# Four-layer residual sequence kernel: the output of the state-space layer and the LSTM's first input group of the next chunk stand one step later in each pass

## The chip, the cores and the metric

The kernel runs on one core of a Trainium2 chip. The metric is device time in microseconds (us). The engines are TensorE (PE; its weight loads are listed on their own as PEld), VectorE (DVE), ScalarE (ACT), GpSimd (POOL) and SyncE (SP), which issues transfers. Each engine takes its own instructions in their written order and waits at semaphores for the others.

## The reference

Four residual layers follow each other on `x` of 4 sequences, 1024 positions, width 512. A conditioning vector per sequence, `cond`, enters layers 0, 1 and 3 and is the start state of layers 0 and 2:

```
x = x + RNN(x, h0=cond)              # h = tanh(x Wx0 + h Wh0), 1024 steps
x = x + SSM(x, cond)                 # short convolution over 4 positions, then
                                     # state = decay*state + dt*B_t*u_t ; y = C_t*state ; y @ Wo + bo
x = x + LSTM(x, h0=cond, c0=0)       # A = x Wx2 + h Wh2 ; i,f,o = sigmoid, g = tanh
                                     # c = f*c + i*g ; h = o*tanh(c), 1024 steps
x = x + x @ (base + lowrank(cond))   # one matrix per sequence
```

The two recurrences make the time serial: the LSTM has 1024 steps, and each needs the state of the one before.

## The kernel before, in words

**Passes and steps.** Positions are cut into 32 chunks of 32. One pass of `do_pass` (line 815) carries the LSTM through the 32 steps of chunk c, while the RNN runs 56 steps ahead of it (`LEAD`). Into the same steps are spread the state-space layer of chunk c+1 (`ssm_jobs`), the RNN's input projection of chunk c+3 (`project0`), the last layer of chunk c-1 (`adapt_jobs`), and the LSTM's input projection (`input_jobs`). The order is written by hand: nothing reorders it.

**The LSTM step.** The hidden width is cut into half A (m = 0) and half B (m = 1). The 96 weight loads and matmuls of `lstm_mm` (line 383; the state is what is loaded, the bfloat16 parts of the weights stream) come in this order: contraction half 0 for A (24), a part for B (8), contraction half 1 for A (24), the rest for B (40). Contraction half 0 reads the state that half A made in the step before; contraction half 1, which begins with the 33rd load, reads the state that half B made. On DVE and ACT follow, per half: `transpose` and `transpose_o` (DVE, 402), `sum` and `sum_o` (DVE, 408), `gates` and `gate_o` (ACT, 415), `products` (DVE, 428), `cell` (DVE, 433), `tanh` (ACT, 438), `h` (DVE, 441) and two `split`s (DVE, 207) that make the lower parts of the state for the bfloat16 products. The `sum` takes in the input projection of the step, which `lstm_input` (ACT, line 390, one copy per half) brings from `xw2` into the tile `tt2` one step ahead.

**The slots.** Around this, each step has three places for other jobs. "pe" is on TensorE between `lstm_mm` and the RNN's matmuls `rnn_mm` (352). "gap" is after B's `cell`, ahead of the two copies of `lstm_input`, of B's `tanh`, `h` and `split`s. "end" is after these and after the RNN's `rnn_pre` (DVE, 367, 368) and `rnn_h` (ACT, 371). So the written order of a step ends like this:

```
Bh.cell()                      # DVE 433
do(t, "gap")
lstm_input(next step, m=0); lstm_input(next step, m=1)     # ACT 390
Bh.tanh()                      # ACT 438
Bh.h(); Bh.split(1); Bh.split(2)                           # DVE 441, 207
rnn_pre(); rnn_h()
do(t, "end")
```

A job is a tuple of step, slot and function. In step 31 the "next step" is step 0 of the next chunk.

**The jobs around the change.** The state-space layer's chain of DVE operations ends with `y` (line 521) in the "end" slot of step 23. `out_mm` (16 matmul calls at line 307 through `tiled`, with 64 contraction rows, out `ssm_out`, bank "po") multiplies it by `Wo`; `x2_end` (DVE, 533, four pieces) adds bias and residual into `x2`, the LSTM's input. `act.copy` (541) keeps the last three positions of `x1` for the next chunk. `input_jobs(c + 1, 0, ...)` then projects `x2` for steps 0 to 7 of the next chunk: four groups of matmuls (`input_mm`, 333, bank "ada"), two turns into `xw2` (`input_turn`, DVE, 337, one for gate groups 0 and 1, one for 2 and 3), and two additions of the bias in place (`input_bias`, DVE, 345, likewise). `lstm_input` reads `xw2` after that. The groups n = 1, 2, 3 for steps 8 to 31 are made inside the chunk's own pass.

Of the kernel before, what the change touches and what calls it, by code (L numbers as in the profile page):

```python
# [16 lines left out]
KC = D // P  # L17
TC = 32
# [21 lines left out]
def cond_resid_kernel(ctx: ExitStack, tc: tile.TileContext, a: dict, out: bass.AP):  # L40
# [410 lines left out]
    def ssm_jobs(c):  # L451
        x, h, po = xin[c % XBUFS], h0[c % 2], {}
        v, act = nc.vector, nc.scalar

        def sm(name):
            return small.tile([NS, TOK], F32, name=name, tag=name, bufs=1)

        def add(ms, t0, t1):
            t = lambda y: y[:, ms, t0:t1].rearrange("p c t b -> p c (t b)")
            v.tensor_add(t(x1[:, :, 3:, :]), t(x), t(h))  # L460


        jobs = [
            (5, "end", lambda: add(slice(0, 2), 0, TC - 4)),
            (6, "end", lambda: add(slice(2, 4), 0, TC - 4)),
            (7, "end", lambda: add(slice(0, 4), TC - 4, TC)),
        ]
        pb = bank("pb", [P, 2, TOK], tag="pb", bufs=1)


        def taps(k):
            for tap in range(TAPS):
                tiled(
                    pb[:, 0, :], lambda j: wp[:, tap, k, CT * j : CT * (j + 1)], x1[:, k, tap : tap + TC, :],
                    tap == 0 and k == 0, tap == TAPS - 1 and k == KC - 1,
                )

        def skip():
            for k in range(KC):
                tiled(  # L480
                    pb[:, 1, :], lambda j: ws[:, k, CT * j : CT * (j + 1)], x1[:, k, 3:, :],
                    k == 0, k == KC - 1, tiles=NS // CT,
                )

        cg, z, e, u, w, p = (sm(n) for n in ("cg", "z", "e", "u", "w", "p"))
        bt, vv, states, y = z, e, w, p
        v3, y3 = (t.rearrange("p (t b) -> p t b", b=B) for t in (vv, states))
        y_last = y3[:, TC - 1, :]
        jobs += [(8 + 2 * k, "pe", lambda k=k: taps(k)) for k in range(KC)]
        jobs.append((16, "pe", skip))  # L490

        def turn(n):
            cols = slice(n * TOK // 4, (n + 1) * TOK // 4)
            v.reciprocal(u[:, cols], u[:, cols])


        jobs += [
            (14, "end", lambda: act.activation(z, pb[:NS, 0, :], AF.Identity, bias=vec[:NS, 0:1])),
            (14, "end", lambda: act.activation(e, pb[:NS, 0, :], AF.Abs, bias=vec[:NS, 0:1])),
            (15, "end", lambda: act.activation(e, e, AF.Exp, scale=-1.0)),  # L500
            (15, "end", lambda: act.activation(u, e, AF.Copy, bias=2.0)),
            (18, "end", lambda: act.activation(cg, pb[NS:, 0, :], AF.Tanh, bias=vec[NS:, 0:1])),
            (18, "end", lambda: v.tensor_mul(u, u, e)),
            (18, "end", lambda: v.tensor_mul(w, u, u)),
            (18, "end", lambda: act.activation(p, w, AF.Copy, scale=2.0 * SERIES[-1])),
            (24, "end", lambda: act.copy(s1, y_last)),
        ]

        chain = [lambda q=q: v.scalar_tensor_tensor(p, p, 2.0 * q, w, ALU.add, ALU.mult) for q in SERIES[-2::-1]]
        chain += [  # L510
            lambda: v.scalar_tensor_tensor(p, p, 2.0, u, ALU.add, ALU.mult),
            lambda: v.scalar_tensor_tensor(bt, z, 0.0, p, ALU.max, ALU.add),
            lambda: v.scalar_tensor_tensor(vv, pb[:NS, 1, :], vec[:NS, 1:2], bt, ALU.add, ALU.mult),
        ]
        for b in range(B):
            chain.append(lambda b=b: v.tensor_tensor_scan(
                y3[:, :, b], decay, v3[:, :, b], s1[:, b : b + 1], ALU.mult, ALU.add
            ))

        chain += [  # L520
            lambda: v.scalar_tensor_tensor(y, states, dt, cg, ALU.mult, ALU.mult),
        ]
        place = lambda n: ("gap", "end", "end")[n % 3]
        jobs += [((16, "end"), (16, "end"), (17, "gap"), (17, "end"))[n] + (lambda n=n: turn(n),) for n in range(4)]
        jobs += [(19 + (n + 1) // 3, place(n + 1), f) for n, f in enumerate(chain)]

        def out_mm():
            po[0] = bank("ssm_out", [P, KC, TOK], tag="po", bufs=1)
            for m in range(KC):
                tiled(po[0][:, m, :], lambda j: wo[:, P * j + CT * m : P * j + CT * (m + 1)], y)  # L530

        def x2_end(m):
            v.scalar_tensor_tensor(
                x2[c % 2][:, m].rearrange("p t b -> p (t b)"), po[0][:, m, :], bo[:, 0, m : m + 1],
                x1[:, m, 3:, :].rearrange("p t b -> p (t b)"), ALU.add, ALU.add,
            )

        jobs += [
            (24, "pe", out_mm),
            *((24 + (m + 1) // 2, ("end", "gap")[m % 2], lambda m=m: x2_end(m)) for m in range(KC)),  # L540
            (26, "end", lambda: act.copy(x1[:, :, 0:3, :], x1[:, :, TC : TC + 3, :])),
        ]
        return jobs

# [270 lines left out]
    def do_pass(c, first=0, src=None, dst=None, last=None):  # L815

        lstm = c >= 0
        jobs = []
        if dst is not None:
            jobs += adapt_jobs(c - 1, dst)  # L820
        if c == NCHUNK - 1:
            more, rest = last_adapt(c, last)
            jobs += more
        if -1 <= c < NCHUNK - 1:
            jobs += ssm_jobs(c + 1)
            jobs += input_jobs(
                c + 1, 0, range(25, 29), ((28, "end"), (29, "gap"), (29, "end"), (30, "gap"))
            )
        if src is not None:
            jobs.append((9, "end", lambda: load_x(c + 4, src)))  # L830
        if c + 3 < NCHUNK:
            for m in range(KC):
                mm, end = project0(c + 3, m)
                t = (18, 20, 22, 30)[m]
                jobs += [(t, "pe", mm), (t, "end", end)]
        if lstm:
            jobs += input_jobs(c, 1, range(4), ((3, "end"), (4, "gap"), (4, "end"), (5, "gap")))
            jobs += input_jobs(c, 2, range(4, 8), ((8, "gap"), (8, "end"), (9, "gap"), (9, "end")))
            jobs += input_jobs(c, 3, range(9, 17, 2), ((15, "end"), (16, "gap"), (18, "gap"), (19, "gap")))

        def do(t, place):
            for slot, where, f in jobs:
                if (slot, where) == (t, place):
                    f()

        for t in range(first, TC):
            r = divmod(c * TC + t + LEAD, TC)
            rnn = r[0] < NCHUNK
            if lstm:
                A, Bh = Half(c, t, 0), Half(c, t, 1)  # L850
                lstm_mm(c, t, 0, 0)
                lstm_mm(c, t, 0, 1, (0, 1))
                lstm_mm(c, t, 1, 0)
                lstm_mm(c, t, 0, 1, (2, 3, 4, 5))
                lstm_mm(c, t, 1, 1)
            do(t, "pe")
            if rnn:
                rnn_mm(*r)
            if c * TC + t < 8 - TC:
                keep_busy()  # L860
            if lstm:
                A.transpose()
                A.sum()
                A.transpose_o()
                A.sum_o()
                A.gates()
                A.products()
                A.gate_o()
                Bh.transpose()
                A.cell()  # L870
                Bh.transpose_o()
                A.tanh()
                Bh.sum()
                Bh.gates()
                A.h()
                Bh.sum_o()
                A.split(1)
                Bh.gate_o()
                Bh.products()
                A.split(2)  # L880
                Bh.cell()
            do(t, "gap")
            if lstm:
                if (c, t) != (NCHUNK - 1, TC - 1):
                    for m in range(2):
                        lstm_input(c if t + 1 < TC else c + 1, (t + 1) % TC, m)
                Bh.tanh()
                Bh.h()
                Bh.split(1)
                Bh.split(2)  # L890
            if rnn:
                rnn_pre(*r)
                rnn_h(*r)
            do(t, "end")
            while later:
                later.pop()()
            for f in early.pop((c, t), ()):
                f()
        if last is not None:
            rest()  # L900
# [78 lines left out]
```

## Time and profile before

| | |
|---|---|
| time, median of 3 runs | 4686.77 us (4686.28 to 4688.5) |
| time of the profiled execution | 4682.72 us |
| span of the profiled execution, first to last instruction | 4680.9 us |
| busy PE / PEld / DVE / ACT / POOL | 4546.1 / 3574.0 / 3951.6 / 1876.8 / 47.9 us |
| granted TensorE clock, mean | 0.998 of full speed |
| DMA, mean over the span | 14 GB/s |

The profiled execution's time is its span and 1.82 us around it. It lies 4.05 us below the median of the runs. Busy time counts instructions that overlap in the pipelines, so a busy PE isn't PE at its peak. The start of half A's `transpose` (line 402, shape 128x192, the first of two such in a step) marks a step in the timeline: from one to the next is the length of the step.

### The profile page before, as it was taken

Reading aid. Unit: us, or ns where it says so; the run is one execution under the profiler, and the core shown is the slowest. Engines: PE = TensorE matmul, PEld = TensorE weight load, DVE = VectorE, ACT = ScalarE, POOL = GpSimd, SP = SyncE. Lnnn points to the kernel's source line nnn. Section 1 sums busy time; section 2 is a strip of 40 time slices with the busy share of each in tenths; the row PEclk is TensorE's granted clock in tenths of the full one; section 3 lists DMA queues with packets and bytes.
Section 4 is the critical chain, followed back from the end, with each engine's and each line's share of the span. In section 5 each row is a group of like instructions: output and inputs, shape, how many; then the busy total and the mean of one; then the engine's idle time right before and its main releaser. Section 6 shows DMA issues by size and latency. Waiting matters only on the chain.

```text
span 4680.9 us, 326427 instructions
## 1 busy us (share of the span) xinstructions
PE 4546.1 (97%) x146816; PEld 3574.0 (76%) x146816; DVE 3951.6 (84%) x22102; ACT 1876.8 (40%) x9693; POOL 47.9 (1%) x92
## 2 busy tenths in 40 slices
PE   7999999999999999999999999999999999999986
PEld 4777777777777777777777777778777777777754
DVE  4688888888888888888888888888888888888876
ACT  3334444444443444443444444444444444444333
POOL 3000000000000000000000000000000000000000
PEclk9999999999999999999999999999999999999999
DMA  6300000000000000000000000000000000000000
GB/s 151 123 6 8 9 7 9 9 7 9 9 7 9 9 7 9 9 7 9 9 7 9 9 7 9 9 7 9 9 7 9 9 7 9 9 5 7 6 6 8
DMA packets 40235, 67.77 MB, mean 14 GB/s; under 512 B 8864, under 2 KB 26016, under 8 KB 38320
## 3 DMA queue, kind: packets, MB, share of 16 engines
q1 hardware_dynamic: 35792, 46.55, 3.7%
q8 instruction: 1147, 18.79, 1.7%
q14 instruction: 256, 2.10, 0.2%
q0 software_dynamic: 1696, 0.19, 0.0%
q10 hardware_dynamic: 1344, 0.14, 0.0%
HBM read 38.34 MB, written 8.39 MB: 10 GB/s over the span
## 4 chain that ended last, share of the span: by engine, by line
PE 91%; DVE 7%; issue 1%; POOL 0%; DMA 0%; ACT 0%; SPq 0%; DVEq 0%; ACTq 0%; POOLq 0%
PE acc L383 55%; PE acc L352 18%; PE proj L333 9%; PE pb L307 3%; DVE tt L402 3%; DVE gc L408 2%; PE proj L307 2%; PE ada L754 2%; DVE prod L428 1%; PE ssm_out L307 1%; DVE h L207 1%; PE idle L307 0%; PE pp L615 0%; DVE h L441 0%; DVE tt L367 0%
## 5 line engine op out<-in xcount | busy, mean ns | idle before, releaser
L383 PE MATMUL acc<-wh,h 128*12 128x256 bf16 x98304 | 2900.4, 273 | 95.0 <-DVE h L207 92.0
L383 PEld LDWEIGHTS <-h 128*12 128x12 bf16 x98304 | 2312.5, 87 | 545.5 <-DVE h L207 181.9
L402 DVE STREAM_TRANSPOSE tt<-acc 128x192 f32<-128x192 f32 (+1 forms) x4096 | 1233.0, 309 | 285.9 <-PE acc L383 261.5
L415 ACT ACTIVATE gc<-gc 128x24 f32<-128x24 f32 (+1 forms) x4096 | 855.3, 216 | 1386.1 <-DVE gc L408 1379.4
L352 PEld LDWEIGHTS acc<-wh,h 128*4 128x4 f32 x32768 | 808.3, 87 | 507.3 <-issue 204.6
L352 PE MATMUL acc<-wh,h 128*4 128x128 f32 x32768 | 1088.6, 273 | 17.3 <-ACT h L371 12.8
L408 DVE TENSOR_REDUCE gc<-tt 128x24 f32<-128x96 f32 (+1 forms) x4096 | 1037.4, 255 | 70.5
L207 DVE TENSOR_TENSOR h<-h 128x8 f32<-128x8 f32 (+1 forms) x4098 | 671.6, 164 | 69.9
L371 ACT ACTIVATE h<-pre 128x16 f32<-128x16 f32 x1024 | 221.5, 216 | 1126.1 <-DVE pre L368 1126.1
L438 ACT ACTIVATE th<-gc 128x8 f32<-128x8 f32 x2048 | 427.7, 209 | 255.1 <-DVE gc L433 220.1
L333 PE MATMUL proj<-wx,x 128*32 128x512 f32 x4096 | 529.6, 592 | 0.0
L441 DVE SCALAR_TENSOR_TENSOR h<-gc,th 128x8 f32<-128x8 f32 x2048 | 328.5, 160 | 143.6 <-ACT th L438 134.0
L367 DVE STREAM_TRANSPOSE tt<-acc 128x128 f32<-128x128 f32 x1024 | 315.4, 308 | 64.7 <-PE acc L352 64.6
L428 DVE SCALAR_TENSOR_TENSOR prod<-gc 128x16 f32<-128x16 f32 x2048 | 347.7, 170 | 12.6
L390 ACT COPY tt<-xw 128x32 f32<-128x32 f32 x2048 | 327.7, 207 | 0.0
L433 DVE SCALAR_TENSOR_TENSOR gc<-prod 128x8 f32<-128x8 f32 x2048 | 297.4, 145 | 0.0
L368 DVE TENSOR_TENSOR pre<-xw,tt 128x16 f32<-128x16 f32 x1024 | 179.6, 175 | 37.6
L307 PE MATMUL proj<-xin,wx 128*32 128x128 f32 x4096 | 135.1, 274 | 12.0 <-DMA wh<-in_Wh_dram 11.9
L307 PE MATMUL pb<-x,wp 128*32 128x128 f32 x4096 | 136.1, 274 | 1.1 <-issue 0.7
L754 PE MATMUL ada<-layer,x 128*32 128x512 f32 (+1 forms) x1056 | 133.9, 586 | 2.7 <-DVE x L747 2.6
L307 PEld LDWEIGHTS proj<-xin,wx 128*32 128x32 f32 x4096 | 114.7, 111 | 15.9 <-DMA wh<-in_Wh_dram 11.9
L333 PEld LDWEIGHTS proj<-wx,x 128*32 128x32 f32 x4096 | 118.8, 110 | 5.5 <-issue 0.3
(125 smaller groups left out, 1161.6 us busy)
## 6 DMA issues: line engine op xcount, KB each, us to landing
layer<-in_w2T_dram SPq DMA_DIRECT2D x32, 512.0 KB, 4.7
xin<-in_xT_dram SPq DMA_DIRECT2D x128, 64.0 KB, 2.5
out_dram<-x SPq DMA_DIRECT2D x124, 64.0 KB, 2.1
wx<-in_Wx_dram SPq DMA_DIRECT2D x20, 256.0 KB, 5.1
layer<-in_Wh_dram SPq DMA_DIRECT2D x16, 256.0 KB, 4.9
wh<-in_Wh_dram SPq DMA_DIRECT2D x4, 256.0 KB, 8.1
layer<-in_w_dram SPq DMA_DIRECT2D x4, 256.0 KB, 4.6
layer<-in_base_dram SPq DMA_DIRECT2D x4, 256.0 KB, 8.7
```

What stands on the lines that cost most here:

```text
L207: nc.vector.tensor_tensor(h[:, :, n], h[:, :, n - 1], upper(h[:, :, n - 1]), ALU.subtract)
L307: nc.tensor.matmul(dst[CT * j : CT * (j + 1)], columns(j), x, start=first, stop=final)
L333: nc.tensor.matmul(ps[CT * j : CT * (j + 1), :], tok, w[:, j], start=(k == 0), stop=(k == KC - 1))
L352: nc.tensor.matmul(acc0[CT * j : CT * j + B, :], h[:, k, (t - 1) % TC, :], wh0[:, k, j * P : (j + 1) * P], start=(k == 0), stop=(k == KC - 1),
L383: nc.tensor.matmul(acc2[mh][CT * j : CT * j + NP * B, :], upper(h[:, k, (t - 1) % TC].rearrange("p s b -> p (s b)")), w[:, :, n0 : n0 + 2 ...
L390: nc.scalar.copy(tt2[m][t % 2][:, :, :, :B], xw2[c % 2][:, :, 2 * m : 2 * m + 2, t, :])
L402: nc.vector.transpose(self.tt[:, g0:g1, :, B:].rearrange("p g c b -> p (g c) b"), acc2[self.m][:, 2 * CT * g0 : 2 * CT * g1],)
L408: nc.vector.tensor_reduce(self.gc[:, to : to + g1 - g0].rearrange("p g c b -> p (g c) b"), self.tt[:, g0:g1, :, : (1 + NP) * B].rearrange( ...
L415: nc.scalar.activation(self.gc[:, g0:g1], self.gc[:, g0:g1], AF.Tanh, scale=0.5)
L428: nc.vector.scalar_tensor_tensor(self.prod, self.gc[:, 0:2], 1.0, self.gc[:, 2:4], ALU.add, ALU.mult)
L438: nc.scalar.activation(self.th, self.c, AF.Tanh, scale=0.5)
L441: nc.vector.scalar_tensor_tensor(self.out[:, :, 0], self.gc[:, 4], 1.0, self.th, ALU.add, ALU.mult)
```

## The change

Everything from `out_mm` to the last `input_bias` of the next chunk's group 0 is written one step later. Nothing is added or removed, and the jobs keep their distances to each other and their slots.

```
         jobs += [
-            (24, "pe", out_mm),
-            *((24 + (m + 1) // 2, ("end", "gap")[m % 2], lambda m=m: x2_end(m)) for m in range(KC)),
-            (26, "end", lambda: act.copy(x1[:, :, 0:3, :], x1[:, :, TC : TC + 3, :])),
+            (25, "pe", out_mm),
+            *((25 + (m + 1) // 2, ("end", "gap")[m % 2], lambda m=m: x2_end(m)) for m in range(KC)),
+            (27, "end", lambda: act.copy(x1[:, :, 0:3, :], x1[:, :, TC : TC + 3, :])),
         ]
...
             jobs += input_jobs(
-                c + 1, 0, range(25, 29), ((28, "end"), (29, "gap"), (29, "end"), (30, "gap"))
+                c + 1, 0, range(26, 30), ((29, "end"), (30, "gap"), (30, "end"), (31, "gap"))
             )
```

| job | before | after |
|---|---|---|
| `out_mm` | 24 pe | 25 pe |
| `x2_end` 0, 1, 2, 3 | 24 end, 25 gap, 25 end, 26 gap | 25 end, 26 gap, 26 end, 27 gap |
| copy of `x1` | 26 end | 27 end |
| `input_mm` 0 to 3 | 25 to 28 pe | 26 to 29 pe |
| `input_turn` (gate groups 0-1, 2-3) | 28 end, 29 gap | 29 end, 30 gap |
| `input_bias` (0-1, 2-3) | 29 end, 30 gap | 30 end, 31 gap |

## The prediction

> **What bounds the kernel now.** I read the page first (busy time, groups), then the timeline of one pass, step by step.
>
> ```profile
> PE 4546.1 (97%) x146816; PEld 3574.0 (76%) x146816; DVE 3951.6 (84%) x22102; ACT 1876.8 (40%) x9693; POOL 47.9 (1%) x92
> ...
> L383 PEld LDWEIGHTS <-h 128*12 128x12 bf16 x98304 | 2312.5, 87 | 545.5 <-DVE h L207 181.9
> ...
> L390 ACT COPY tt<-xw 128x32 f32<-128x32 f32 x2048 | 327.7, 207 | 0.0
> ```
>
> PE looks like the bound: 97% busy. The second row adds that the LSTM's weight loads were held up for 545.5 us, most of all by `split` (207), the end of the recurrence. The last row will matter: `lstm_input`'s 2048 copies never held ACT up (0.0 us idle before them).
>
> Now steps 30 and 31 of a pass in the middle. Columns: start, duration, engine, line, operation, count; in brackets the engine's idle time before it and what ended that.
>
> ```profile
> 2415.59 0.38 DVE L402 STREAM_TRANSPOSE tt<-acc 128x192 f32<-128x192 f32 x1 [0.17 <-PE acc L383]
> ...
> 2416.35 0.88 PEld L307 LDWEIGHTS proj<-xin,wx 128*32 128x32 f32 x32
> ...
> 2417.86 0.32 ACT L390 COPY tt<-xw 128x32 f32<-128x32 f32 x2
> ...
> 2418.01 0.17 DVE L433 SCALAR_TENSOR_TENSOR gc<-prod 128x8 f32<-128x8 f32 x1
> 2418.09 0.42 DVE L345 TENSOR_TENSOR xw<-xw,b 128x256 f32<-128x256 f32 x1
> ...
> 2418.21 0.21 ACT L438 ACTIVATE th<-gc 128x8 f32<-128x8 f32 x1
> 2418.45 0.17 DVE L441 SCALAR_TENSOR_TENSOR h<-gc,th 128x8 f32<-128x8 f32 x1
> 2418.65 0.37 DVE L207 TENSOR_TENSOR h<-h 128x8 f32<-128x8 f32 x2
> ...
> 2419.96 0.38 DVE L402 STREAM_TRANSPOSE tt<-acc 128x192 f32<-128x192 f32 x1 [0.50 <-PE acc L383]
> ...
> 2423.03 0.37 DVE L207 TENSOR_TENSOR h<-h 128x8 f32<-128x8 f32 x2
> 2423.45 1.63 PEld L383 LDWEIGHTS <-h 128*12 128x12 bf16 x64 [0.21 <-DVE h L207]
> 2424.34 0.38 DVE L402 STREAM_TRANSPOSE tt<-acc 128x192 f32<-128x192 f32 x1 [0.51 <-PE acc L383]
> ```
>
> Step 30 starts at 2415.59, step 31 at 2419.96, step 0 of the next chunk at 2424.34: 4.37 and 4.38 us. Step 30 carries a job of 32 loads on PE, step 31 none, and they are equally long; so PE's work doesn't set the length. The last rows show what does: B's second `split` ends at 2423.40 (2423.03 + 0.37), the 33rd load (the first that reads B's state) starts 0.05 later after 0.21 idle, and the next step begins 0.94 after that `split`. Measured load by load, the 33rd load starts 0.054 us after B's `split` in nearly every step, and the widest gap between loads, 0.228 at the median, stands there in 928 of 1015 steps. So B's chain `cell`, `tanh`, `h`, two `split`s is the path, without slack, with or without a job on PE.
>
> Step 30's "gap" job (345, 2418.09 to 2418.51) costs nothing today: it runs on DVE while B's `tanh` runs on ACT. That holds because nothing on ACT waits for it; the copies had started at 2417.86.
>
> One step is longer, step 24:
>
> ```profile
> 2388.82 0.34 DVE L521 SCALAR_TENSOR_TENSOR p<-w,sp,cg 64x128 f32<-64x128 f32 x1
> ...
> 2389.10 0.38 DVE L402 STREAM_TRANSPOSE tt<-acc 128x192 f32<-128x192 f32 x1
> ...
> 2390.07 0.81 PEld L307 LDWEIGHTS ssm_out<-p,wo 64*32 64x32 f32 x32 [0.22 <-DVE tt L402]
> ...
> 2391.08 0.77 PEld L352 LDWEIGHTS acc<-wh,h 128*4 128x4 f32 x32 [0.20 <-ACT th L438]
> ...
> 2393.70 0.38 DVE L402 STREAM_TRANSPOSE tt<-acc 128x192 f32<-128x192 f32 x1 [0.47 <-PE acc L383]
> ```
>
> The next step starts 4.60 later. Over the passes the median is 4.605 against 4.378 for its neighbours: 0.227 us more.
>
> **The change part by part.**
>
> *Moved on PE: `out_mm` from step 24 to 25, `input_mm` from 25-28 to 26-29.* The same 32 + 4 x 8 loads a pass, one step later. The tempting reading is that step 24 waits for `y` and that a step more frees 0.227 us a pass: 31 x 0.227 = 7.0 us gained. The rows speak against it: `y` (521) ends at 2389.16, and `out_mm` starts at 2390.07, 0.91 later, behind `lstm_mm` as any PE job does. What differs is that it starts 0.97 us after the step's first row, where other jobs start at 0.76 (2416.35 - 2415.59), and `rnn_mm` behind it sits idle for 0.20 again. The releasers named in the brackets are only the nearest events in time; the built order has `out_mm` wait for `y` alone. `out_mm` alone has 64 contraction rows (its loads are 64x32; all others here are 128 rows). The Trainium skill, "TensorEngine Tiling (Array Packing)", section "Tiling Modes", says that a change of the tiling mode drains TensorE. By this rule the 0.2 on both sides belongs to `out_mm` and moves with it: step 24 falls to 4.38, step 25 rises to 4.60, sum 0. By the wait reading the sum is -7.0. I take 0, since the row has `y` ready 0.91 us early.
>
> *Moved on DVE: four `x2_end` (0.34 each), two turns (0.44), two bias additions (0.42); on ACT the copy of `x1`.* Same slots, so the same cover: a "gap" job lies under B's `tanh`, an "end" job in the 0.5 us in which DVE waits for PE ahead of each step (2419.96: [0.50]). If that cover were gone the eight would cost up to 3.1 us a pass, but only the one below meets anything new. The banks "po" and "ada" are still read empty by step 30; their next takers come in steps 0 and 4 of the next pass. None of the moved jobs issues a transfer; SP's and POOL's queues don't change.
>
> *What becomes late: the second bias addition.* In step 31 its "gap" slot stands directly ahead of `lstm_input` for step 0 of the next chunk, which reads exactly what it writes. In the built order ACT gets a separate wait there, 31 times, ahead of both copies, for the count that this addition raises; B's `tanh` has no wait of its own any more. Before, neither copy waited for DVE. ACT takes its work in order, so B's `tanh`, which needs only `cell`, is queued behind two copies that wait for the addition; `h`, both `split`s and PE's 33rd load wait for it in turn. Costed with step 30's rows, from B's `cell` (2418.01):
> - addition ends: 2418.51, at +0.50;
> - DVE's end to ACT's start: 0.033 (medians of `sum` to `gates` and `cell` to `tanh`);
> - the separate wait: 0.02, the shortest such row on DVE (line 345's semaphore waits took 21 to 50 ns);
> - two copies: 0.107 from start to start (all 1024 pairs), and I take 0.11 again to `tanh` (ACT's next operation after 371 starts 0.12 later);
> - `tanh` starts at 0.50 + 0.033 + 0.02 + 0.107 + 0.11 = +0.77, in place of +0.20 (2418.21): 0.57 late.
>
> Bounds: without a price for the wait, 0.55; with copies that don't overlap (0.207 each, as long as they last) and a wait of 0.05, 0.80. A gain is excluded: no row gets earlier. I take 0.57, the nearest to the pair spacing measured. Since B's chain has no slack, all of it lengthens step 31, to 4.95. Before the first LSTM step nothing is lost: ACT is behind `rnn_h` of that step anyway, which follows the addition on DVE.
>
> *Sum.* Chunks 0 to 30 hand over to a next one: 31 x 0.57 = +17.7 us; bounds +17.1 and +24.8. Against the profiled execution: 4682.72 + 17.7 = 4700.4. The median of the runs stands 4.05 above that execution (4686.77), so the forecast is 4686.77 + 17.7 = 4704.5.
>
> **The rivals.**
> 1. *Step 24's excess is a wait after all and goes.* For it: PE's idle time ahead of `out_mm` exists, 0.22 us. Against: `y` is ready 0.9 us before in nearly every pass. Time: 4686.77 + 17.7 - 7.0 = 4697.5.
> 2. *Not slower: PE's queue absorbs B's delay.* Place: the 33rd load. If PE, busy 97%, were behind by then, a late B would cost nothing; it decides as soon as PE is 0.57 us behind B's `split` there, 31 times. For: the page's 97%, and pass 0, where PE has more to do and steps last up to 5.4 us. Against: the load starts 0.05 after `split`, with a gap before it, in over nine steps of ten. Time: 4686.8, or 4679.8 if rival 1's gain comes with it.
> 3. *The copies don't overlap after a wait.* 31 x 0.80: 4711.6. For: copies can wait for an earlier ACT result. Against: the spacing was 0.107 in every pair. It is inside my case's range.
>
> That the change doesn't do what it says can be left out: the written order is what is built, and the new wait stands in it.
>
> **How the numbers follow.** My case 0.87 (rival 3 included), rival 1 0.06, rival 2 0.07. What a measurement of this kernel can tell from no change is about 0.2%, 9.4 us, so slower begins at 4696.1. My case and rival 1 lie above it: 0.93. Rival 2 is within 0.2% on both its values: 0.06, and 0.01 is left for a gain over 0.2% that no row supports. The range runs from rival 1's 4697.5, with the 1 us by which runs differ below it, to my upper bound's 4711.6: 4696.5 to 4712.0.
>
> **What would show it.** Right: step 24 near 4.38, step 25 near 4.60, step 31 near 4.95; ACT idle before line 390 of about 31 x 0.6 = 19 us, ended by DVE, where it was 0.0; B's `tanh` in step 31 0.77 after `cell`; `tanh` to `h` unchanged (0.24). Rival 1: step 25 at 4.38. Rival 2: copies late, but step 31 at 4.38. Rival 3: 0.2 between copies. I'm wrong if step 31 stays at 4.38, or if a step other than 24, 25 and 31 changes by over 0.02.

## The result, and the profile after

| | before | changed |
|---|---|---|
| median of 7 runs each | 4688.5 us (4684.02 to 4690.81) | 4705.51 us (4700.92 to 4706.49) |
| ratio to before, 95% interval | | 1.0038 (1.0028 to 1.0048) |
| profiled execution: time, span | 4682.72, 4680.9 us | 4700.92, 4699.1 us |

The changed kernel is slower by 17.0 us in the medians and by 18.2 us between the two profiled executions. The forecast was 17.7 us more, 4704.5 us, counted from the median of the three runs of before known then, 4686.77.

The page shows it in the groups by line. The row for `h` of both halves was, in the kernel before:

```profile
L441 DVE SCALAR_TENSOR_TENSOR h<-gc,th 128x8 f32<-128x8 f32 x2048 | 328.5, 160 | 143.6 <-ACT th L438 134.0
```

In the changed kernel these are the rows for the LSTM's weight loads, for `h`, and for the copies of `lstm_input`:

```profile
L383 PEld LDWEIGHTS <-h 128*12 128x12 bf16 x98304 | 2309.7, 87 | 573.1 <-DVE h L207 218.1
...
L441 DVE SCALAR_TENSOR_TENSOR h<-gc,th 128x8 f32<-128x8 f32 x2048 | 330.5, 161 | 161.8 <-ACT th L438 152.0
...
L390 ACT COPY tt<-xw 128x32 f32<-128x32 f32 x2048 | 328.4, 207 | 20.4 <-DVE xw L345 20.3
```

Read them from the bottom up. The copies, which never held ACT up before (0.0 us), now do so for 20.4 us, released by the bias addition (345). DVE's idle time ahead of `h` grew from 143.6 to 161.8 us, and the loads' idle time from 545.5 to 573.1, still released by `split`. That is one delay, handed from ACT to DVE to PE. The loads' growth of 27.6 us holds more than it: step 31 gives 31 x (0.84 - 0.21) = 19.5 us of it, by the rows below. Busy times moved by 6 us at most.

In the timeline, step 31 of a pass in the middle (columns as before: start, duration, engine, line, operation, count, and in brackets the idle time before):

```profile
2429.74 0.17 DVE L433 SCALAR_TENSOR_TENSOR gc<-prod 128x8 f32<-128x8 f32 x1
2429.82 0.42 DVE L345 TENSOR_TENSOR xw<-xw,b 128x256 f32<-128x256 f32 x1
...
2430.33 0.34 ACT L390 COPY tt<-xw 128x32 f32<-128x32 f32 x2 [0.66 <-DVE xw L345]
2430.57 0.21 ACT L438 ACTIVATE th<-gc 128x8 f32<-128x8 f32 x1
2430.81 0.17 DVE L441 SCALAR_TENSOR_TENSOR h<-gc,th 128x8 f32<-128x8 f32 x1 [0.57 <-ACT th L438]
2431.01 0.37 DVE L207 TENSOR_TENSOR h<-h 128x8 f32<-128x8 f32 x2
...
2431.43 1.63 PEld L383 LDWEIGHTS <-h 128*12 128x12 bf16 x64 [0.84 <-DVE h L207]
...
2432.32 0.38 DVE L402 STREAM_TRANSPOSE tt<-acc 128x192 f32<-128x192 f32 x1 [0.50 <-PE acc L383]
```

B's `cell` ends at 2429.91. Nothing but `cell` is needed for `tanh`, yet it starts at 2430.57, behind the two copies, which wait for the addition that ends at 2430.24. The 33rd load then waits 0.84 us, where it had waited 0.21. It still starts 0.05 after B's last `split` (2431.38), and the next step 0.94 after it: B's chain had no slack.

Step 25 of that kernel:

```profile
2400.80 0.38 DVE L402 STREAM_TRANSPOSE tt<-acc 128x192 f32<-128x192 f32 x1 [0.50 <-PE acc L383]
...
2401.76 0.81 PEld L307 LDWEIGHTS ssm_out<-p,wo 64*32 64x32 f32 x32 [0.22 <-issue]
...
2402.77 0.77 PEld L352 LDWEIGHTS acc<-wh,h 128*4 128x4 f32 x32 [0.20 <-ACT th L438]
...
2405.40 0.38 DVE L402 STREAM_TRANSPOSE tt<-acc 128x192 f32<-128x192 f32 x1 [0.47 <-PE acc L383]
```

`out_mm` has the same idle 0.22 ahead of it and 0.20 behind it, with `y` finished more than a whole step before. The long step moved along with it.

In this one step of a pass it is PE that is late, and not B's chain. Load by load in this trace, the 33rd load of the next step starts 0.18 us after B's last `split` (median over 27 passes), with 0.001 idle ahead of it; in each of the 31 other steps of a pass it starts 0.05 after, with 0.12 us idle or more. In the kernel before, the same holds one step earlier. So of `out_mm`'s 0.42 us of idle time on PE a part falls into a wait for B that was there anyway, and the step is longer by 0.22 only.

Length of the steps, from A's `transpose` to the next, median over 27 passes (us):

| step | before | changed |
|---|---|---|
| 24 | 4.605 | 4.386 |
| 25 | 4.371 | 4.604 |
| 30 | 4.381 | 4.387 |
| 31 | 4.379 | 5.005 |

Between the two profiles step 31 gives +19.8 us in the sum over all passes, steps 24 and 25 give -6.6 and +7.3, and all other LSTM steps +5.1: 0.9 of it in the first pass, 1.0 in the one step behind the last hand-over, the rest 0.003 a step on average. The stretch ahead of the first LSTM step was 6.0 us shorter in the changed kernel's profile, and the last step with what follows it 1.4 us. The first of these is spread: over the seven kernels profiled here, one execution each, the stretch lasted 151.8 to 158.9 us, and the edits don't sort it (152.7 to 156.0 in three kernels built on the changed one, 153.0 and 158.9 in two built on the one before).

### The profile page after: what moved, and what is told of

The parts are those of the page before. It is cut to its first block, busy times and chain, and to the rows that moved or that the text cites. A ratio compares the mean times of both kernels' runs of the same rounds, so it can differ in the third digit from the quotient of the medians.

```text
span 4699.1 us, 326456 instructions
## 1 busy us (share of the span) xinstructions
PE 4549.1 (97%) x146816; PEld 3570.0 (76%) x146816; DVE 3957.3 (84%) x22102; ACT 1878.5 (40%) x9693; POOL 47.9 (1%) x92
## 4 chain that ended last, share of the span: by engine, by line
PE 87%; DVE 10%; issue 1%; ACT 1%; POOL 0%; DMA 0%; SPq 0%; DVEq 0%; ACTq 0%; POOLq 0%
PE acc L383 53%; PE acc L352 17%; PE proj L333 9%; DVE tt L402 3%; DVE gc L408 3%; PE pb L307 3%; PE proj L307 2%; PE ada L754 2%; DVE h L207 1%; DVE prod L428 1%; PE ssm_out L307 1%; DVE h L441 1%; DVE gc L433 0%; DVE tt L367 0%; PE idle L307 0%
## 5 line engine op out<-in xcount | busy, mean ns | idle before, releaser
L383 PEld LDWEIGHTS <-h 128*12 128x12 bf16 x98304 | 2309.7, 87 | 573.1 <-DVE h L207 218.1
L441 DVE SCALAR_TENSOR_TENSOR h<-gc,th 128x8 f32<-128x8 f32 x2048 | 330.5, 161 | 161.8 <-ACT th L438 152.0
L390 ACT COPY tt<-xw 128x32 f32<-128x32 f32 x2048 | 328.4, 207 | 20.4 <-DVE xw L345 20.3
L307 PEld LDWEIGHTS proj<-xin,wx 128*32 128x32 f32 x4096 | 115.6, 111 | 15.6 <-issue 13.1
```

Of the source, the lines that this page charges most:

```text
L307: nc.tensor.matmul(dst[CT * j : CT * (j + 1)], columns(j), x, start=first, stop=final)
L383: nc.tensor.matmul(acc2[mh][CT * j : CT * j + NP * B, :], upper(h[:, k, (t - 1) % TC].rearrange("p s b -> p (s b)")), w[:, :, n0 : n0 + 2 ...
L390: nc.scalar.copy(tt2[m][t % 2][:, :, :, :B], xw2[c % 2][:, :, 2 * m : 2 * m + 2, t, :])
L441: nc.vector.scalar_tensor_tensor(self.out[:, :, 0], self.gc[:, 4], 1.0, self.th, ALU.add, ALU.mult)
```

## The experiments

Times in one row were taken on the same chip; the ratio is to the kernel before. The medians are of 5 to 21 runs, those of before of 49 (last row: 12); the steps are medians over 27 passes of one profile.

| kernel | median, us | before, us | ratio (95%) | step 24 / 25 / 30 / 31, us |
|---|---|---|---|---|
| B's `tanh` first | 4683.8 | 4682.39 | 1.0004 (0.9997 to 1.0010) | 4.38 / 4.60 / 4.38 / 4.38 |
| one addition alone | 4702.25 | 4682.39 | 1.0045 (1.0032 to 1.0057) | 4.61 / 4.38 / 4.38 / 5.01 |
| `out_mm` on 128 rows | 4675.88 | 4682.39 | 0.9987 (0.9980 to 0.9993) | 4.38 / 4.38 / 4.39 / 4.38 |
| both additions at step 30's end | 4684.63 | 4682.39 | 1.0004 (0.9996 to 1.0012) | 4.38 / 4.60 / 4.47 / 4.37 |
| short addition | 4695.88 | 4684.96 | 1.0023 (1.0012 to 1.0034) | 4.39 / 4.60 / 4.39 / 4.77 |

**B's `tanh` ahead of the copies.** The changed kernel, with two calls exchanged in step 31:

```
+                if t == TC - 1:
+                    Bh.tanh()
                 if (c, t) != (NCHUNK - 1, TC - 1):
...
-                Bh.tanh()
+                if t < TC - 1:
+                    Bh.tanh()
```

> The changed kernel, except that in step 31 B's tanh (438) is issued ahead of the two copies of lstm_input (390). The copies still wait for the bias addition of step 31. Theory (B's tanh is late only because it is queued on ACT behind the copies): step 31 falls from 5.00 to 4.38 us, step 25 stays at 4.60, the time goes back to that of the kernel before, about 4687 (19 below the changed kernel). Rival A (the next chunk's input itself comes too late, so that the first sums wait for it) and rival B (the addition holds up B's h on DVE): step 31 stays near 5.00, time near 4705.

Its step 31, and the head of the next:

```profile
2427.22 0.17 DVE L433 SCALAR_TENSOR_TENSOR gc<-prod 128x8 f32<-128x8 f32 x1
2427.31 0.42 DVE L345 TENSOR_TENSOR xw<-xw,b 128x256 f32<-128x256 f32 x1
...
2427.43 0.21 ACT L438 ACTIVATE th<-gc 128x8 f32<-128x8 f32 x1 [0.26 <-DVE gc L433]
2427.67 0.17 DVE L441 SCALAR_TENSOR_TENSOR h<-gc,th 128x8 f32<-128x8 f32 x1
2427.82 0.34 ACT L390 COPY tt<-xw 128x32 f32<-128x32 f32 x2 [0.18 <-DVE xw L345]
...
2429.17 0.38 DVE L402 STREAM_TRANSPOSE tt<-acc 128x192 f32<-128x192 f32 x1 [0.50 <-PE acc L383]
2429.66 0.33 DVE L408 TENSOR_REDUCE gc<-tt 128x24 f32<-128x96 f32 x1
```

The copies are as late as in the changed kernel (0.60 after `cell`'s start here, 0.59 there) and wait for the same addition; only `tanh` no longer stands behind them. They end at 2428.16, 1.50 ahead of the `sum` that reads them. Step 31 is back at 4.376 us. So it was the order in ACT's queue, neither the late input data nor the addition's time on DVE, and both rivals fall. One other step isn't quite as before: step 0 of the next chunk takes 4.458 us in place of 4.375. Its first `sum` (408) starts 0.49 after `transpose`, elsewhere 0.42. The trace of this kernel has a separate wait on DVE ahead of that `sum`, 32 times, where the changed kernel has one.

**One addition alone.** The kernel before, with one number changed:

```
-                c + 1, 0, range(25, 29), ((28, "end"), (29, "gap"), (29, "end"), (30, "gap"))
+                c + 1, 0, range(25, 29), ((28, "end"), (29, "gap"), (29, "end"), (31, "gap"))
```

> The kernel before, with one job alone moved: the second bias addition from step 30's gap to step 31's gap. Theory: the whole cost of the change is in this move: step 24 stays at 4.60, step 31 rises from 4.38 to 5.00, 31 x 0.62 = 19 us, time about 4706. Rival (the later out_mm, input_mm or turns have a part in it): step 31 rises by less, or the time stays clearly below 4704.

Its row for the copies, among the groups by line, is the changed kernel's:

```profile
L390 ACT COPY tt<-xw 128x32 f32<-128x32 f32 x2048 | 328.5, 207 | 20.4 <-DVE xw L345 20.3
```

Step 24 stays at 4.605 and step 31 takes 5.008. The time is 19.9 us above before in the medians. The whole cost is in this one move, to within the interval (15 to 27 us); the other moved jobs have no part in it that a run here could tell.

**`out_mm` on 128 rows.** The kernel before, with 64 rows of zeros under `y` and `Wo`:

```
-    wo = const.tile([NS, D], F32, name="wo", tag="wo")
+    wo = const.tile([P, D], F32, name="wo", tag="wo")
+    p128 = const.tile([P, TOK], F32, name="p128", tag="p128")
...
+    nc.vector.memset(wo[NS:], 0.0)
+    nc.vector.memset(p128[NS:], 0.0)
...
-        cg, z, e, u, w, p = (sm(n) for n in ("cg", "z", "e", "u", "w", "p"))
+        cg, z, e, u, w = (sm(n) for n in ("cg", "z", "e", "u", "w"))
+        p = p128[:NS]
...
-                tiled(po[0][:, m, :], lambda j: wo[:, P * j + CT * m : P * j + CT * (m + 1)], y)
+                tiled(po[0][:, m, :], lambda j: wo[:, P * j + CT * m : P * j + CT * (m + 1)], p128)
```

> The kernel before, with out_mm on 128 contraction rows: y and Wo get 64 rows of zeros below (set once at the start), so that out_mm has the same shape on PE as all its neighbours. Same number of matmuls, same result. Theory (the 0.2 us ahead of out_mm and behind it come from its 64 rows): step 24 falls from 4.60 to 4.38, 31 x 0.227 = 7 us less, about 4680. Rival (they come from a wait for y, or from the bank that out_mm writes): step 24 stays at 4.60, time near 4687.

Its step 24 (its lines stand 3 or 4 further down: 525 is `y`, 405 `transpose`, 310 `out_mm`, 355 `rnn_mm`):

```profile
2383.38 0.34 DVE L525 SCALAR_TENSOR_TENSOR p<-w,sp,cg 64x128 f32<-64x128 f32 x1
...
2383.65 0.38 DVE L405 STREAM_TRANSPOSE tt<-acc 128x192 f32<-128x192 f32 x1
...
2384.41 0.89 PEld L310 LDWEIGHTS ssm_out<-p,wo 128*32 128x32 f32 x32
...
2385.28 0.86 PEld L355 LDWEIGHTS acc<-wh,h 128*4 128x4 f32 x32
...
2388.03 0.38 DVE L405 STREAM_TRANSPOSE tt<-acc 128x192 f32<-128x192 f32 x1 [0.24 <-PE acc L386]
```

`y` ends at the same place (0.07 after the step's start), `out_mm` writes the same bank, and it does twice the rows. Yet it starts 0.76 after the step's start like every other job, and the idle 0.22 and 0.20 are gone. So they come with the 64 rows. Single loads show how (medians over 27 passes): here, and at the job of step 30 in the kernel before, the first load of a job starts 0.01 us before the last matmul of the group ahead of it. With 64 rows `out_mm`'s first load starts 0.20 after that matmul's start, and `rnn_mm`'s first load 0.20 after `out_mm`'s last matmul: where the number of rows changes, PE's loads no longer run ahead of its matmuls. No step is left in which the 33rd load starts later than 0.05 after B's `split` (by the same medians). The step is 4.384, 0.221 less, 6.9 us over 31 passes; measured are 6.5 us less. This kernel has the lowest ratio of those run and is ahead of both the kernel before and the changed one; its interval lies wholly below 1.

**Both additions in step 30's end slot.** The changed kernel:

```
-                c + 1, 0, range(26, 30), ((29, "end"), (30, "gap"), (30, "end"), (31, "gap"))
+                c + 1, 0, range(26, 30), ((29, "end"), (30, "gap"), (30, "end"), (30, "end"))
```

> The changed kernel, with the second bias addition in step 30's end slot, behind the first, in place of step 31's gap. Nothing is then late for the copies: step 31 at 4.38. But the end slot holds two additions. DVE is idle for 0.50 us ahead of the next step without such a job and for 0.17 with one addition, so a second takes 0.33 where 0.17 is left: step 30 at 4.38 + 0.16 to 0.25, 5 to 8 us in all, about 4692 to 4695. Rival (the step has slack on DVE behind half A): step 30 stays at 4.38, time about 4687.

```profile
2417.99 0.75 DVE L345 TENSOR_TENSOR xw<-xw,b 128x256 f32<-128x256 f32 x2
...
2418.66 0.38 DVE L402 STREAM_TRANSPOSE tt<-acc 128x192 f32<-128x192 f32 x1
```

Step 31 is free of the wait, and step 30 takes 4.469, 0.09 longer than the 4.38 before and not 0.16 to 0.25. The sign was right and the size was not. That two additions in a row take 0.75 us and not 2 x 0.42 stood in the lower value already (0.33 for the second); left out was that the next `transpose` starts 0.08 before the second is over, which makes 0.33 - 0.17 - 0.08 = 0.08. 31 x 0.09 is 2.8 us, and the medians differ by 2.2; the interval holds 1, so the times alone couldn't tell it.

**A short addition.** The changed kernel, with the second addition cut in two:

```
-    def input_bias(c, n, g):
+    def input_bias(c, n, g, t0=0, t1=TG):
...
-            lambda: input_bias(c, n, 0), lambda: input_bias(c, n, 2),
+            lambda: input_bias(c, n, 0), lambda: input_bias(c, n, 2, 0, TG if n else 1),
+            lambda: input_bias(c, n, 2, 1),
...
-                c + 1, 0, range(26, 30), ((29, "end"), (30, "gap"), (30, "end"), (31, "gap"))
+                c + 1, 0, range(26, 30), ((29, "end"), (30, "gap"), (30, "end"), (31, "gap"), (31, "end"))
```

> The changed kernel, with the second bias addition cut in two: in step 31's gap only the columns of step 0, the one step that the next copies read (32 elements a partition in place of 256), the other seven in step 31's end slot. Theory (the price is the time from B's cell to the end of the addition that the copies wait for, plus the wait and the copies ahead of tanh): an addition of 32 elements lasts about 0.17 us as B's other short DVE operations do, in place of 0.42, so tanh starts 0.25 earlier than in the changed kernel: step 31 about 4.75, 31 x 0.37 = 11.5 over the kernel before, time about 12 less the run-to-run spread above it. Rival (a fixed price of the separate wait, whatever it waits for): step 31 stays near 5.00, 19 above.

```profile
2428.89 0.17 DVE L433 SCALAR_TENSOR_TENSOR gc<-prod 128x8 f32<-128x8 f32 x1
2428.97 0.18 DVE L345 TENSOR_TENSOR xw<-xw,b 128x32 f32<-128x32 f32 x1
...
2429.24 0.34 ACT L390 COPY tt<-xw 128x32 f32<-128x32 f32 x2 [0.42 <-DVE xw L345]
2429.49 0.20 ACT L438 ACTIVATE th<-gc 128x8 f32<-128x8 f32 x1
2429.72 0.17 DVE L441 SCALAR_TENSOR_TENSOR h<-gc,th 128x8 f32<-128x8 f32 x1 [0.57 <-ACT th L438]
```

The addition takes 0.18 in place of 0.42, `tanh` starts 0.60 after `cell`'s start in place of 0.83, and step 31 takes 4.770 in place of 5.005. The times follow: 10.9 us above before. The addition became 0.24 shorter and the step 0.235: the price followed the length of what the copies wait for, one to one.

## Why the prediction was right, point by point

*Where the time goes.* As forecast: one step a pass, step 31, through ACT's queue (20.4 us of idle time ahead of the copies, where about 19 was forecast). Exchanging the order on ACT takes the cost away, moving that one addition alone brings all of it, and shortening the addition shortens it. These three together show the cause.

*The size.* Step 31 came out at 5.005 us where 4.95 was forecast: 0.626 late, not 0.57. Term by term, from `cell`'s start, medians over the passes:

| term | forecast | measured |
|---|---|---|
| end of the addition | 0.50 | 0.504 |
| from there to the first copy, with the separate wait | 0.033 + 0.02 | 0.088 |
| first copy to `tanh` | 0.107 + 0.11 | 0.243 |
| `tanh` starts at | 0.77 | 0.835 |

Two terms were too small: the way through the separate wait (0.088 for 0.053), and the copies (0.243 for 0.217). The trace has the wait itself as a row:

```profile
L390 ACTq EVENT_SEMAPHORE  x31: 17/17/17, 306.2 to 4547.8; - x31
```

Such a wait starts 0.031 us after the addition's end (median) and lasts 0.017, so the sum had both prices nearly right; the first copy starts another 0.040 behind it, a term that the sum put at nothing. The second copy follows the first by 0.124 us and not by 0.107, and `tanh` the second by 0.119. The short addition gave the same, 0.089 and 0.242, so neither depended on how long the addition was. Copies that don't overlap would have stood 0.207 apart, so rival 3 is out.

*The sum.* 31 x 0.626 is 19.4 us by step 31 alone, and the single addition measured 19.9; the forecast had 17.7. That the changed kernel itself came out at +17.0 is within the noise: its 95% interval is +13.1 to +22.5 us. The agreement to a microsecond is luck; the agreement of step 31 (0.57 for 0.626) is not, since it rests on terms that were measured one by one.

*Step 24 (rival 1).* It fell by 0.219 us and step 25 rose by 0.233, as the drain would have it: no gain. The prediction rested this on the row that has `y` ready 0.91 us early, and on a rule of the Trainium skill, "TensorEngine Tiling (Array Packing)", section "Tiling Modes", against the reading as a wait. The 128-row kernel bears it out for the number of rows: same place, same data ready, no idle time. The loads that no longer run ahead (0.20 us on both sides) are what a drain would look like; no run here varies the tiling in any other way. One thing the prediction had too simply: in the step behind `out_mm` PE is late by its own work, so B's chain is not the path "with or without a job on PE" there.

*PE's queue as a cushion (rival 2).* The 33rd load waited 0.84 us in place of 0.21 and started 0.05 after `split` as ever. PE at 97% busy gave no cushion at this step. (The longest step of pass 0 in the kernel before lasted 5.93 us, not 5.4.)

*"Any other step changes by over 0.02".* None did at the median, apart from 24, 25 and 31. Single steps did: in passes 3 to 28 some moved by up to 0.5 us up or 0.4 down, in pass 0, where other work fills PE, by up to 0.8 up and 0.3 down. Step 31 of pass 0 rose by only 0.36 us, from 4.642 to 4.998: it had been long already. In pass 29 step 31 took 5.196: between the first copy and `tanh` lay 0.43 us in place of 0.24, and the same in the kernels with the single and with the short addition (0.44 and 0.43). In the changed kernel's profile step 31 of pass 30 and the step behind it took 5.39 and 5.38; in the kernel with the single addition 4.99 and 4.38. What these two passes met stays open; together it is under 2.5 us.

## What to carry to other kernels

Before moving a job to a later slot, look at what stands directly behind that slot in every queue, not only on the job's own engine: a reader that now has to wait blocks everything behind it there, even what doesn't need it. Where the two calls could be exchanged, the cost went. An engine that is 97% busy need not be the one that sets the time: find the chain whose last link releases the next step with no gap. And a step that is longer at the same job in every pass may be paying for the job's shape and not for a wait: moving it only moves the cost, and padding it to its neighbours' shape took 0.2 us a pass away here.

## What the runs showed of the hardware that was not expected

- A separate wait on ACT ahead of an instruction cost more than its own length: from DVE's end to the first copy 0.088 us (0.089 with the short addition), where a wait that the instruction itself carries takes 0.033. The wait's own row lasts 0.017 of it, and 0.040 pass between its end and the copy. On DVE, in the kernel with `tanh` first, such a row ahead of the `sum` lasts 0.021, the `sum` starts 0.044 behind it and 0.07 later than without it.
- A matmul job with 64 contraction rows among jobs with 128 cost 0.22 us ahead and 0.20 behind on PE, of which 0.22 us showed in the step's length; the same job with twice the rows, half of them zeros, left its step as long as the others (4.384 us).
- Two bias additions in a row took 0.75 us where one takes 0.42, and the next DVE instruction started 0.08 us before the second had ended.
